# Expert rows turned by DMA transposes as two float16 numbers, instead of by TensorE

## The chip, the cores and the metric

The kernel runs on one core of one Trainium2 chip. The metric is the device time of one execution in microseconds (us), smaller being better. Engines are named as in the profile: PE is TensorE (PEld its weight loads), DVE is VectorE, ACT is ScalarE, POOL is GpSimd, SP is SyncE. `L1262` is line 1262 of the kernel.

## The reference: what is computed

Two layers on 4096 nodes of 256 features. Each layer adds graph attention (one round in the first layer, two in the second) and then a feed-forward part to its input, each on normalised rows. The change lies in the last part alone, a mixture of six experts of which each row takes its best two:

```
rh = relu(features @ router_w1 + router_b1)
expert_logits = softmax(rh @ router_w2 + router_b2)
top_w, top_i = top_k(expert_logits, 2)
routing_weights = softmax(top_w)
h1 = relu(features @ expert_w1[e] + expert_b1[e])
h2 = relu(h1 @ expert_w2[e] + expert_b2[e])
expert_out = h2 @ expert_w3[e] + expert_b3[e]
x = x + sum over the two chosen e of expert_out * routing_weights
```

All inputs are float32; weights of an expert are three 256 x 256 matrices.

## The kernel before

The program is one long sequence of stages: an attention layer with mask making, a feed-forward stage of 30 steps (from about 814 to 1793 us), two more attention layers (to about 3087), a router (to about 3162), the expert loop (to about 3392), and a last pass that gathers the results and adds them up. Instructions outside the attention loops and the feed-forward stage are ordered by a scheduler, engine by engine, when the program is built: the order in the source is a wish, the data and the buffers of the pools decide.

**Router** (L987 to L1215). In eight groups of 512 rows it normalises rows, writes them to a DRAM table `nd` (L1015), transposes them on TensorE, and computes the six logits (L1001, L1024). In between SP issues the loads of the expert weights, `ew` (L1036). VectorE then makes from the logits a list: the 8192 pairs of row and expert, grouped by expert into T = 37 tiles of TR = 256 places. `source` says which row of `nd` stands in each place, `dest` where its result goes in the DRAM table `yd`, `expert` which expert a tile belongs to.

**Expert loop** (L1305 to L1325), over the 37 tiles. For tile i:

- `gather` (L1224): two indirect DMAs, issued by POOL, bring 2 x 128 rows of `nd` into `gx` (four buffers).
- `turn` (L1234): four float32 transposes on TensorE into PSUM (`pt`), and one VectorE copy to `xT` (L1241), 128 x 512.
- `fetch` (L1243): the tile's expert number goes into registers of PE, DVE and ACT, and the weights of layers one and two are copied from `ew` to `w0` (VectorE) and `w1` (ScalarE), both L1255, 128 x 512, three buffers each.
- `hidden(i, 0)` (L1257): four float32 matmuls (each is two records in the trace), then bias and relu by ScalarE in two halves (L1273) to `h0`.
- `hidden(i, 1)`: the same with `w1`, bias and relu by VectorE (L1275) to `h1`.
- `result` (L1277): four float32 matmuls with `ew[2]`, the addition of the bias by VectorE into `ye` (L1291, three buffers), and two indirect DMAs by POOL to `yd` (L1293).

In the built order TensorE runs, from tile to tile: second product of i, first product of i+1, last product of i, transposes of i+2. POOL has the gathers of seven tiles ahead of the first scatter and then takes gathers and scatters in turn. Each POOL DMA waits for the eighth before it to have landed.

**The feed-forward stage** is not changed, but it holds the operations that the change uses. Half of its product is made from pairs of float16 numbers: ScalarE rounds the scaled numbers to float16 (L852), VectorE subtracts that from the scaled numbers and rounds what is left (L853), a DMA transpose issued by SP turns both halves at once (L857), and TensorE multiplies every half of the rows with every half of the weights (L899), while the other half of its columns is float32 (L896).

## Time and profile before

| | us |
|---|---|
| median of 3 runs | 3432.09 (3427.78 to 3432.75) |
| the profiled execution's own time | 3432.09 |
| its span, first to last instruction | 3430.3 |
| TensorE, busy in the span | 3156.7 (92%) |
| VectorE | 3115.3 (91%) |
| ScalarE | 2754.3 (80%) |
| GpSimd | 1242.3 (36%) |
| first gather issued | 3162.7 |
| first product of tile 0 begins | 3170.0 |
| last scatter issued | 3392.0 |

How to read the lines that follow. A group line reads: line, engine, operation, output <- inputs, shape, count, then busy us and mean ns of one, then the idle time of the engine just before these instructions and what ended it. Timeline lines begin with start and length in us. Matmuls are pipelined: the start of the next tells more than the modelled end. TensorE's granted clock is 1.00 through the whole expert loop and 0.50 in most of the second half of the router.

### The profile page before, as it was taken

To read this page: it belongs to the slowest core of one execution; us is meant where nothing else is said; L and a number is where in the kernel's file an instruction comes from. 1 tells how busy PE (TensorE), PEld (TensorE's weight loads), DVE (VectorE), ACT (ScalarE), POOL (GpSimd) and SP (SyncE) were. 2 spreads that over 40 slices of the span, in tenths; PEclk is the share of its full clock that TensorE was granted. 3 is DMA by queue.
4 is the path that set the end of the run, shared out by engine and by line. 5 is a ranking of instruction groups with operands and counts; after the bars stand their busy time and mean duration, and the time that the engine had idled before them with its cause. 6 is when DMAs were issued, how large, how long until landed. Compare 5 with 4: busy or idle time off the path is not lost.

```text
span 3430.3 us, 84143 instructions
## 1 busy us (share of the span) xinstructions
PE 3156.7 (92%) x34367; PEld 2771.3 (81%) x34367; DVE 3115.3 (91%) x6016; ACT 2754.3 (80%) x3414; POOL 1242.3 (36%) x1149
## 2 busy tenths in 40 slices
PE   7889999996999999999988999999989999985995
PEld 4788888884888888888876999999779999983884
DVE  7999999998999999999988999999889999996445
ACT  3888888896888888888866999999799999982221
POOL 3211100003999999999992000000200000002662
PEclk9999999997999999999999999999999999996997
DMA  7997886603333333333354031230503041314224
GB/s 146 173 228 152 184 184 142 192 22 77 68 67 68 69 69 69 69 69 68 67 140 147 22 123 58 90 118 24 167 24 124 27 136 43 120 46 145 88 91 185
DMA packets 533658, 351.62 MB, mean 103 GB/s; under 512 B 350589, under 2 KB 483866, under 8 KB 533274
## 3 DMA queue, kind: packets, MB, share of 16 engines
q1 hardware_dynamic: 452210, 287.12, 30.4%
q0 software_dynamic: 73920, 52.97, 9.9%
q10 hardware_dynamic: 7144, 6.16, 0.6%
q8 instruction: 271, 4.44, 0.5%
q14 instruction: 113, 0.93, 0.1%
HBM read 248.01 MB, written 68.81 MB: 92 GB/s over the span
## 4 chain that ended last, share of the span: by engine, by line
PE 36%; DVE 35%; issue 13%; POOL 7%; ACT 6%; DMA 2%; DVEq 0%; POOLq 0%; ACTq 0%; SPq 0%
DVE m L617 17%; PE acc L569 10%; PE po L899 9%; PE po L896 9%; ACT st L483 4%; DVE rows L632 3%; PE tp L831 2%; DVE m L632 2%; POOL th L862 2%; PE ph L1262 1%; POOL yd L1293 1%; DVE z_st L874 1%; DVE y L838 1%; POOL gx L1227 1%; DVE u L496 1%
## 5 line engine op out<-in xcount | busy, mean ns | idle before, releaser
L569 PE MATMUL acc<-vals,m 128*128 128x130 f16 (+1 forms) x19456 | 1722.4, 233 | 72.0 <-DVE m L632 42.5
L483 ACT ACTIVATE st<-f1b,f2b 128x1024 bf16<-128x1024 f32 (+2 forms) x1664 | 1659.1, 1073 | 98.8 <-DVE m L617 92.1
L569 PEld LDWEIGHTS <-m 128*128 128x128 bf16 x19456 | 1517.3, 98 | 170.2 <-DVE m L632 64.8
L617 DVE TENSOR_TENSOR m<-st,m 128x2048 bf16<-128x2048 bf16 (+2 forms) x832 | 929.1, 1134 | 15.2 <-ACT st L483 14.9
L569 PE MATMUL acc<-vals,rows 128*128 128x130 f16 x5120 | 614.1, 221 | 15.1 <-DVE rows L632 15.1
L899 PE MATMUL po<-w,zT 128*128 128x256 f16 x3840 | 580.4, 274 | 5.7 <-DMA zT<-z 5.7
L896 PE MATMUL po<-wT,zT 128*128 128x256 f32 x1920 | 579.1, 384 | 6.4 <-ACT zT L881 6.4
L862 POOL TENSOR_TENSOR th<-th,y 128x1024 f32<-128x1024 f32 x240 | 568.8, 2370 | 38.4 <-ACT th L861 14.8
L899 PEld LDWEIGHTS <-zT 128*128 128x128 f16 x3840 | 377.6, 98 | 169.7 <-DMA zT<-z 7.3
L569 PEld LDWEIGHTS <-rows 128*128 128x128 bf16 x5120 | 490.0, 96 | 20.5 <-DVE rows L632 20.1
L632 DVE TENSOR_TENSOR rows<-m,m 128x2048 bf16<-128x2048 bf16 x320 | 391.7, 1224 | 10.2
L838 DVE SCALAR_TENSOR_TENSOR y<-po,z_rs,bias 128x256 f32<-128x256 f32 x928 | 384.8, 477 | 4.2 <-PE po L899 2.1
L874 DVE BATCH_NORM_STATS2 z_st<-z 128x6 f32<-128x256 f32 x960 | 335.5, 412 | 0.0
L896 PEld LDWEIGHTS po<-wT,zT 128*128 128x128 f32 x1920 | 292.5, 193 | 16.4 <-ACT zT L881 7.8
L106 POOL TENSOR_TENSOR ln_rstd<-ln_rstd,mhalf 128x4 f32<-128x4 f32 x32 | 42.1, 1317 | 656.8 <-DVE ln_rstd L105 641.9
L850 ACT ACTIVATE z<-th 128x1024 f32<-128x1024 f32 x240 | 251.2, 1046 | 7.3 <-POOL th L862 6.6
L209 POOL DMA_DIRECT2D rows<-in_adj_dram x80 | 72.9, 912 | 492.9 <-PE tp_m L219 479.4
L861 ACT ACTIVATE th<-y 128x1024 f32<-128x1024 f32 x240 | 249.8, 1041 | 0.1
L885 POOL TENSOR_TENSOR z_rs<-z_rs,mhalf 128x4 f32<-128x4 f32 x240 | 244.5, 1019 | 0.0
L881 ACT COPY zT<-tp 128x512 f32<-128x512 f32 x240 | 140.8, 587 | 116.2 <-PE tp L831 116.2
L632 DVE TENSOR_TENSOR m<-m,m 128x1792 bf16<-128x1792 bf16 (+1 forms) x200 | 202.2, 1011 | 13.0 <-PE acc L569 0.5
L462 POOL MEMSET hs<- 128x4 f32 x3 | 0.3, 103 | 582.4 <-DVE u L513 582.3
(246 smaller groups left out, 3159.1 us busy)
## 6 DMA issues: line engine op xcount, KB each, us to landing
m<-edges SPq DMA_DIRECT2D x32, 2048.0 KB
rows<-in_adj_dram POOLq DMA_DIRECT2D x64, 448.0 KB
edges<-ms SPq DMA_DIRECT2D x64, 448.0 KB
m<-edges SPq DMA_DIRECT2D x16, 1792.0 KB
f1b<-fd SPq DMA_DIRECT2D x32, 512.0 KB
rows<-x1d SPq DMA_DIRECT2D x16, 512.0 KB
y<-yd SPq DMA_DIRECT2D x16, 512.0 KB
f1b<-fd SPq DMA_DIRECT2D x16, 448.0 KB
```

Source lines behind the costliest of these rows:

```text
L483: nc.scalar.activation(steps[at][:, s, :w], f1b[c, h][:, :w], AF.Relu, bias=f2b[:, 2 * q + s, h : h + 1], scale=BIG)
L569: nc.tensor.matmul(acc[:, i, cols], lhs[:, s, rows], v[:, cols], start=(j == 0 and n_ == 0), stop=(j == NT - 1 and n_ == 1), skip_group_ch ...
L617: nc.vector.tensor_tensor(m1[:, :, :w], st[:, :, :w], m, OP.logical_and if turned(q) else OP.min)
L632: nc.vector.tensor_tensor(m2[:, :, :w], m, m1[:, :, :w], OP.subtract)
L838: nc.vector.scalar_tensor_tensor(y[:, g * G + r, :], po[:, r, :], rstd[:, r : r + 1], last if end else bias, op0=OP.mult, op1=OP.add,)
L850: nc.scalar.activation(z, th.pop(u), AF.Silu, scale=0.01)
L861: nc.scalar.activation(th[at], y[:, g * G : (g + 1) * G, :], AF.Tanh, scale=0.01)
L862: ins = nc.gpsimd.tensor_tensor(th[at], th[at], y[:, g * G : (g + 1) * G, :], OP.add)
L874: nc.vector.bn_stats(st[:, r, :], z[:, r, :])
L885: nc.gpsimd.tensor_tensor(rs[u], rs[u], mhalf, OP.pow)
L896: nc.tensor.matmul(po[:, r, :], src[:, r * P : (r + 1) * P], wT, start=True, stop=False)
L899: nc.tensor.matmul(po[:, r, :], src16[:, part * G + r, :], w16[:, other, :], start=False, stop=(part == 1 and other == 1),)
```

## The change

It is confined to the router's set-up and the expert loop.

- Router: the greatest absolute value of the first layer's weights is found (six reductions of 128 x 512 on VectorE, a transpose and a small matmul on TensorE, five small VectorE instructions). From its exponent come two powers of two in `wscale`: one by which weights are scaled ahead of the rounding, one that takes that scale and the rows' scale of 2^10 out again.
- `turn`: no TensorE transposes, no copy of `xT`. ScalarE writes the scaled rows, rounded to float16, into the first half of `x16`; VectorE writes what the rounding left into the second half; SP issues one DMA transpose of all 128 x 1024 numbers into `xT`. `x16` has three buffers, `xT` four. PSUM's pool for the transposes goes.
- `fetch`: ScalarE and VectorE make two float16 halves of the first layer's weights in the same way, in place of VectorE's copy; the copy of the second layer's weights stays.
- `hidden(i, 0)`: sixteen float16 matmuls of 128 x 256 in place of four float32 ones (two halves of rows by two of weights, by two parts of the inner sum, by two of the output); relu takes `wscale` as its scale.
- The loop: `gather` is asked for three tiles ahead in place of two, with five `gx` buffers in place of four; `turn` two tiles ahead in place of one.

```diff
+            far = rone.tile([P, E + 1], F32, name="far")
+            for e in range(E):
+                nc.vector.tensor_reduce(
+                    far[:, e : e + 1],
+                    ew[0][:, e].rearrange("p k c -> p (k c)"),
+                    axis=AX.X, op=OP.max, apply_absolute_value=True,
+                )
+            nc.vector.tensor_reduce(far[:, E:], far[:, :E], axis=AX.X, op=OP.max)
+            ps = bank("ps_s")
+            nc.tensor.transpose(ps[:1, :P], far[:, E:], ident)
+            big = rone.tile([1, 1], F32, name="big")
+            nc.vector.tensor_reduce(big, ps[:1, :P], axis=AX.X, op=OP.max)
+            ps = bank("ps_s")
+            nc.tensor.matmul(ps[:, :1], ones[:1, :], big, start=True, stop=True)
...
         def gather(i):
-            rows[i] = work.tile([P, 2, C], F32, name="gx", bufs=4)
+            rows[i] = work.tile([P, 2, C], F32, name="gx", bufs=5)
...
         def turn(i):
             src = rows.pop(i)
-            pt = ps_t.tile([P, KC, TR], F32, name="pt")
-            for k in range(KC):
-                for r in range(2):
-                    nc.tensor.transpose(pt[:, k, r * P : (r + 1) * P], src[:, r, k * P : (k + 1) * P], ident)
-            xT[i] = work.tile([P, KC, TR], F32, name="xT")
-            nc.vector.tensor_copy(xT[i], pt)
+            x16 = work.tile([P, 2, 2, C], F16, name="x16")
+            nc.scalar.activation(x16[:, 0], src, AF.Copy, scale=ZS)
+            nc.vector.scalar_tensor_tensor(x16[:, 1], src, ZS, x16[:, 0], op0=OP.mult, op1=OP.subtract)
+            xT[i] = work.tile([P, 8, P], F16, name="xT", bufs=4)
+            nc.sync.dma_start_transpose(xT[i], x16.rearrange("p s r c -> p (s r c)"))
...
         def fetch(i):
...
-            held[i] = []
-            for layer, copy in enumerate((nc.vector.tensor_copy, nc.scalar.copy)):
-                held[i].append(work.tile([P, KC, C], F32, name=f"w{layer}"))
-                copy(held[i][layer], ew[layer][:, bass.DynSlice(which[i], 1)].rearrange("p o k c -> p (o k) c"))
+            w16 = work.tile([P, 2, KC, C], F16, name="w0")
+            nc.scalar.activation(w16[:, 0], first, AF.Identity, scale=wscale[:, :1])
+            nc.vector.scalar_tensor_tensor(
+                w16[:, 1], first, wscale[:, :1], w16[:, 0], op0=OP.mult, op1=OP.subtract
+            )
+            held[i] = [w16, work.tile([P, KC, C], F32, name="w1")]
+            nc.scalar.copy(held[i][1], second)
 
         def hidden(i, layer, src):
...
+            if layer == 0:
+                src = src.rearrange("p (s r k) n -> p s k r n", s=2, k=KC)
+                ops = [(w[:, v, k], src[:, u, k]) for k in range(KC) for v in range(2) for u in range(2)]
+            else:
+                ops = [(w[:, k], src[:, k]) for k in range(KC)]
...
-        gather(0)
-        gather(1)
+        for i in range(3):
+            gather(i)
         for i in range(T + 1):
-            if i + 2 < T:
-                gather(i + 2)
+            if i + 3 < T:
+                gather(i + 3)
             if i < T:
                 if i == 0:
                     fetch(0)
                     turn(0)
+                    turn(1)
...
-            if i + 1 < T:
-                turn(i + 1)
+            if i + 2 < T:
+                turn(i + 2)
```

In the prediction, "high half" is ScalarE's rounding and "low half" VectorE's rest; `h0` and `h1` are the outputs of the first two products; "first", "second" and "last product" of a tile are `hidden(i, 0)`, `hidden(i, 1)` and the matmuls of `result(i)`.

## The prediction

> **What bounds the kernel now.** The edit touches one stage at the end, so I first placed that stage in the chain of work that ended last, then took busy times in stretches of it. From 3186 to 3386 us the expert loop runs steadily (stretch, its length, then busy time and count of PE, PEld, DVE, ACT, POOL, then granted clock, DMA share, GB/s):
>
> ```profile
> 3236.00:3286.00 50.00, 49.01 (x240) 41.87 (x239) 21.95 (x43) 12.77 (x27) 34.13 (x35) 1.00 0.28 92
> 3286.00:3336.00 50.00, 48.62 (x238) 41.25 (x237) 22.71 (x44) 12.28 (x25) 32.97 (x34) 1.00 0.27 88
> ```
>
> TensorE is 98% busy at full clock; VectorE and ScalarE are under half. The order of time on TensorE (start, length) gives the price of a tile; `ph<-xT` is the first product, `ph<-h` the second, `po` the last, `pt` the transposes:
>
> ```profile
> 3201.75 1.89 PE L1283 MATMUL po<-ew,h 128*128 x8
> 3203.48 0.60 PE L1239 MATMUL pt<-ident,gx 128*128 128x128 f32 x4
> 3203.91 1.89 PE L1262 MATMUL ph<-h,w 128*128 128x256 f32 x8
> 3206.08 1.99 PE L1262 MATMUL ph<-xT,w 128*128 128x256 f32 x8 [0.27 <-DVE xT L1241]
> 3207.91 1.89 PE L1283 MATMUL po<-ew,h 128*128 x8
> 3209.63 0.60 PE L1239 MATMUL pt<-ident,gx 128*128 128x128 f32 x4
> 3210.07 1.89 PE L1262 MATMUL ph<-h,w 128*128 128x256 f32 x8
> 3211.80 1.89 PE L1262 MATMUL ph<-xT,w 128*128 128x256 f32 x8
> 3213.53 0.81 PE L1283 MATMUL po<-ew,h 128*128 x3
> ```
>
> Read the starts, since ends overlap. A product of four float32 matmuls (eight records) holds TensorE 1.73 us (3211.80 to 3213.53), four transposes 0.43 (3203.48 to 3203.91). A tile is 3 x 1.73 + 0.43 = 5.62 us (3207.91 to 3213.53); every other tile adds 0.54 for transposes that are copied late (3201.75 to 3207.91 is 6.16). From the end of tile 1's last product (3186.46) to that of tile 36 (3389.41) are 202.95 us. POOL is the near second: 1.27 to 1.35 us from one DMA issue to the next, four a tile, about 5.3 (busy us and mean ns, then idle before and what ended it):
>
> ```profile
> L1293 POOL DMA_INDIRECT yd<-ye,dest x67 | 67.4, 1006 | 27.1 <-issue 16.0 <-DVE ye L1291 6.5 <-DVE xT L1241 4.6
> L1227 POOL DMA_INDIRECT gx<-nd,source x60 | 59.0, 982 | 38.9 <-PE pt L1239 21.1 <-issue 17.8
> L1255 ACT COPY w<-ew 128x512 f32 x32 | 19.8, 618 | 93.8 <-PE ph L1262 48.4 <-issue 45.4
> L1255 DVE COPY w<-ew 128x512 f32 x31 | 15.3, 493 | 36.2 <-PE ph L1262 36.2
> ```
>
> The new operations stand in the feed-forward stage, which does the same trick on tiles of the same shape:
>
> ```profile
> 1700.16 0.60 PE L899 MATMUL po<-w,zT 128*128 128x256 f16 x4
> 1700.59 0.60 PE L896 MATMUL po<-wT,zT 128*128 128x256 f32 x2
> ```
>
> and, with least, median and most ns of one,
>
> ```profile
> L852 ACT ACTIVATE z<-z,scale x240: 721/722/724, 818.6 to 1777.2; 128x512 f16<-128x512 f32 x120
> L853 DVE SCALAR_TENSOR_TENSOR z<-z,scale,z x240: 741/742/2062, 819.3 to 1778.9; 128x512 f16<-128x512 f32 x120
> L857 SPq DMA_TRANSPOSE zT<-z x240: 1232/1233/2364, 820.1 to 1784.7; - x120
> ```
>
> Four float16 passes hold TensorE 0.43 us, 0.109 each. The transpose occupies SP 1.23 us, but by the trace's semaphore records it is 3.04 us from issue to the sixteenth landing (median of 240; least 3.01; 4.43 at the 95th per cent and 5.37 at most, where bulk loads share its queue).
>
> **What the Trainium skill says.** "TensorE: Matmul & The Clock Gate", Back-to-back issue gap: an isolated warm matmul takes N/2.4 + 2.5 ns, 109 ns for N = 256; the 0.109 here agrees. Same page, What's actually happening: an idle window of about 3.4 us halves the clock. Agrees: it is 0.5 from 3126.9 to 3174.6. "DMA: Bandwidth & Descriptors", Queues, rings and completion order: each DMA engine takes turns between queues by whole packets. The trace of before never has a transpose beside an indirect DMA, so it can't confirm it. "SBUF — State Buffer", SBUF: two separate sides: a float32 SBUF copy on VectorE locks the port by which GpSimd writes descriptors. Agrees in size: POOL's issue takes 0.945 us while VectorE does little (3173 to 3177), 0.98 to 1.01 in the loop.
>
> **The change part by part**, per tile unless said.
>
> 1. TensorE. Four transposes go: -0.43, and the 0.54 stall of every second tile. The first product becomes 16 float16 passes: 16 x 0.109 = 1.74 against 1.73, nothing. New floor: 1.73 + 1.73 + 1.74 = 5.20.
>
> 2. ScalarE gains two roundings. The weights' takes 0.72 (L852's row). The rows' has no strided source: between the 0.59 of a plain 128x512 copy (L881) and 0.72; I take 0.66. In all 0.84 + 0.72 + 0.66 + 0.62 = 2.84 of 5.2. VectorE loses xT (0.68) and the copy of w (0.49) and gains two subtractions, 0.74 by L853, 0.68 by the float32 one of L673; I take 0.70 for the rows': 3.0 a tile. As work both are hidden under TensorE. Their order is not.
>
> 3. The new ring. In the built program's order VectorE has, per tile i: h1(i), weights' low half (i+4), ye(i), rows' low half (i+8). ScalarE has h0(i), weights' high (i+3), rows' high (i+7), w1(i+3). The three x16 buffers make the rows' high half of tile i+8 wait for the transpose of tile i+5; the four xT buffers make that wait until the first product of tile i+1 is done. Behind the waiting ScalarE instruction stand w1(i+4) and h0(i+2); behind VectorE's stand h1(i+1), and TensorE's last product (i+1) waits for it. SP has nothing else queued. From the end of the first product (i+1): to SP 0.30 (ScalarE's h0 started at 3267.01 where TensorE's next product started at 3266.75: 0.26), transpose 3.04, to ScalarE 0.10, high half 0.66, to VectorE 0.06, low half 0.70, first half of h1 0.48 less 0.08 overlap, to TensorE 0.06: 5.32. Then last product (i+1), second (i+2), first (i+2 to i+3): 5.20. That is two tiles in 10.52, 5.26 a tile. So the ring is longer than TensorE's work even with a quiet transpose.
>
> 4. The transpose beside gathers and scatters, not shown before. A gather is 32 packets of 4 KB, two per DMA engine at 0.2 us each (L1227's and L1293's DMA share 0.27 over 4 per tile gives 0.4 us each). Bounds: nothing extra (3.04), or as under bulk loads (4.43). It cannot be below nothing: extra traffic doesn't speed it. During its 1.4 us of moving bytes POOL starts about one DMA, so I take +0.4: two tiles in 10.92, 5.46 each. The ring applies to last products 2 to 29 (rows end at 37): 28 x 5.46 = 152.9; then six at 5.20 and 4.2 for the last (before: 3385.21 to 3389.41): 188.3. Against 202.95: **-14.6**.
>
> 5. Gathers three ahead, five buffers. The built order puts 26 gathers ahead of the first scatter (before: 14). 26 x 1.25 from 3162.75 ends near 3195; three ye buffers cover it, since ye(3) is due after 3200. POOL needs 4 x 1.25 to 1.30 = 5.0 to 5.2: under 5.46. Without that cover POOL would set 5.3.
>
> 6. Start of the loop. Row gathers land at 3167.05 and then every 2.5 us (before's trace). ScalarE's order puts the high halves of tiles 0 to 5 ahead of h0(0). Tile 5 lands near 3179.6, so h0(0) ends near 3181.1; the second product (0) began at 3174.8 before. VectorE's h1(0) also stands behind tile 6 (lands near 3182), h1(1) behind tile 8 (near 3187). Tile 1's last product then ends near 3191.1 instead of 3186.46: +4.6; with the 5 us gap cooling the clock near 3193.1: +6.7. Taken: **+5.6**.
>
> 7. Router. Six 128x512 reductions (0.67 by L160's) on VectorE, in gaps that GpSimd's power leaves or beside TensorE's chain; the transpose of far makes TensorE's router product (6) wait for VectorE, about 0.9. All exposed would be 4 + 0.9; all but that wait hidden 0.9. Taken **+1.2**. The scaling is ready 35 us before use: free, covered by routing.
>
> Sum: -14.6 + 5.6 + 1.2 = -7.8. The profiled execution took 3432.09, 1.79 round its span of 3430.3, and equals the median: 3424.3, say **3424**.
>
> **Rivals.** (a) The ring has slack, TensorE sets 5.20: for it, the transposes in the FFN keep to 3.04, hand-overs may be shorter; against, the queue order. 28 x 0.26 less: 3417. (b) *Slower*: gathers and scatters stretch the transpose, at one place, T between x16 and xT. Every 1 us adds 0.5 x 28 = 14 us. It breaks even at 3.04 + 0.4 + 7.8/14 = 4.0 us, and is slower by 0.2% (6.9 us, about what a measurement here can tell from no change) from 4.5; at 4.6, 3440. For it: 4.43 under bulk; against: only 0.27 of DMA time is taken. (c) A wash: TensorE gets its 0.7 a tile back and the ring returns it, at 5.6 to 5.75 a tile (192.2 to 196.4 in place of 188.3), with a cold start and up to 3.7 more in the router: 3429 to 3437.
>
> **How the numbers follow.** Forecast 0.50, its own range 3420 to 3429, three fifths of it faster by over 0.2% (0.30), the rest within (0.20). (a) 0.17, faster. (c) 0.13, within. (b) 0.20, slower. So faster 0.47, within 0.33, slower 0.20. Leaving out little below 3414 and half of (b)'s tail above 3440 gives 3414 to 3440.
>
> **What would show it.** Right: TensorE's last products 5.4 to 5.5 us apart, waiting 0.2 to 0.3 on VectorE's h (L1314); ScalarE's x16 waiting on the transpose; transposes landing 3.3 to 3.6 us after issue; TensorE idle near 3176 to 3181; last seven tiles at 5.2. Wrong: transposes at 4 us or over (b), no wait ahead of the last product (a), POOL without gaps.

## The result, and the profile after

The changed kernel takes 3462.13 us in the median of six runs (3459.25 to 3473.58), the kernel before 3432.85 beside it (3427.78 to 3434.89): ratio 1.0095, 95% interval 1.0077 to 1.0114. It is slower by about 1%, outside the forecast range. The profiled execution took 3459.25, its span is 3457.5, so 27.2 more than before.

The same two stretches of the expert loop, in the changed kernel (stretch, length, then busy time and count of PE, PEld, DVE, ACT, POOL, granted clock, DMA share, GB/s):

```profile
3236.00:3286.00 50.00, 43.40 (x240) 34.58 (x240) 22.30 (x38) 20.58 (x37) 30.90 (x31) 0.97 0.47 121
3286.00:3336.00 50.00, 44.40 (x271) 37.00 (x269) 22.52 (x39) 21.77 (x40) 33.20 (x33) 1.00 0.53 127
```

TensorE, 98% busy before, is now busy 87 and 89%: it has less work a tile and waits more. The order of time on TensorE shows where:

```profile
3211.41 2.00 PE L1322 MATMUL po<-ew,h 128*128 x8 [1.70 <-DVE h L1314]
3213.24 1.89 PE L1301 MATMUL ph<-h,w 128*128 128x256 f32 x8
3214.97 1.91 PE L1301 MATMUL ph<-xT,w 128*128 128x256 f16 x16
3216.72 1.89 PE L1322 MATMUL po<-ew,h 128*128 x8
3218.45 1.89 PE L1301 MATMUL ph<-h,w 128*128 128x256 f32 x8
3220.17 1.91 PE L1301 MATMUL ph<-xT,w 128*128 128x256 f16 x16
3223.54 2.06 PE L1322 MATMUL po<-ew,h 128*128 x8 [1.46 <-DVE h L1314]
```

Sixteen float16 passes hold TensorE 1.75 us (3214.97 to 3216.72), as forecast, and every second tile waits for VectorE's `h1` ahead of its last product, as forecast; but the wait is 1.5 to 1.7 us in these lines (0.7 to 1.7 in tiles 2 to 8) and not 0.2 to 0.3. The groups of the loop from 3186 to 3386 (busy us and mean ns, then idle before and what ended it):

```profile
L1332 POOL DMA_INDIRECT yd<-ye,dest x60 | 61.5, 1026 | 58.0 <-DVE ye L1330 45.5 <-issue 12.5
L1256 POOL DMA_INDIRECT gx<-nd,source x56 | 57.8, 1032 | 21.6 <-issue 17.4 <-DVE x L1267 4.2
L1285 DVE SCALAR_TENSOR_TENSOR w<-ew,wscale,w 128x512 f16<-128x512 f16 x31 | 23.3, 751 | 64.6 <-ACT w L1284 39.6 <-PE po L1322 12.4 <-ACT h L1312 10.4
L1284 ACT ACTIVATE w<-ew,wscale 128x512 f16 x31 | 22.2, 716 | 0.0
L1267 DVE SCALAR_TENSOR_TENSOR x<-gx,x 128x512 f16<-128x512 f32 x30 | 20.8, 694 | 31.3 <-ACT x L1266 17.9 <-DMA gx<-nd,source 6.9 <-issue 6.4
L1266 ACT ACTIVATE x<-gx 128x512 f16<-128x512 f32 x30 | 18.9, 630 | 56.7 <-DMA xT<-x 44.0 <-DMA gx<-nd,source 9.8 <-DVE ye L1330 2.9
```

The prices are those of the forecast (0.716 and 0.630 on ScalarE, 0.751 and 0.694 on VectorE), and the rows' high half waits for the transpose, 44.0 us in 200. Where the loss lies, from the starts of the last products (tile 0, 1, 27, 36):

| | before | after |
|---|---|---|
| first gather issued | 3162.75 | 3161.59 |
| tile 0's last product starts | 3178.8 | 3192.6 |
| tile 1's | 3184.6 | 3204.3 |
| tile 27's | 3337.4 | 3367.6 |
| tile 36's | 3387.7 | 3413.7 |
| mean from tile 1 to 27 | 5.88 | 6.28 |

The start loses 19.7 us, tiles 1 to 27 another 10.5, and the last nine win 4.2 back (eight at 5.2 to 5.3 us, the last at 4.2). Two things lie behind this: the first 27 tiles wait for slow transposes (step 4 below), and at the start something else, which is seen nowhere in the forecast. All engines of the changed kernel, 3181 to 3199 us (PE's weight loads and most of POOL's rows left out):

```profile
3181.00 3.78 PE L1301 MATMUL ph<-h,w 128*128 128x256 f32 x8 [4.29 <-ACT h L1312]
...
3184.58 1.72 PE L1301 MATMUL ph<-xT,w 128*128 128x256 f16 x10
...
3187.80 0.94 POOL L1256 DMA_INDIRECT gx<-nd,source  x1 [0.30 <-issue]
3189.05 0.94 POOL L1256 DMA_INDIRECT gx<-nd,source  x1 [0.30 <-issue]
3190.30 0.94 POOL L1256 DMA_INDIRECT gx<-nd,source  x1 [0.30 <-issue]
3191.54 0.94 POOL L1256 DMA_INDIRECT gx<-nd,source  x1 [0.30 <-issue]
3192.08 0.62 ACT L1289 COPY w<-ew 128x512 f32 x1 [8.61 <-remote]
3192.08 0.88 DVE L1314 TENSOR_SCALAR h<-ph,bsel 128x256 f32<-128x256 f32 x2 [7.89 <-remote]
...
3192.62 3.54 PE L1322 MATMUL po<-ew,h 128*128 x8 [6.31 <-DVE h L1314]
...
3198.47 1.02 ACT L1312 ACTIVATE h<-ph,bsel,wscale 128x256 f32<-128x256 f32 x2 [5.24 <-remote]
```

Tile 0's second product has ended by 3184.8. VectorE's relu and ScalarE's copy wait for nothing but that, and start together 7.3 us later. The profile finds no releaser ("remote"), because at that moment nothing ends: TensorE's count, which both wait for, is raised only then (3192.05 by the trace's semaphore records). Tile 1's first product ends at 3186.3; its relu and the next transpose start, and VectorE's wait for it ends, all at 3198.46, 12.1 us later. From here on I call this a **late signal**. In the stretch from 3160 us to the last product, 15 of TensorE's 92 recorded raises come over 0.1 us after their product's end; of VectorE's 154 and ScalarE's 133 none does. In the kernel before it is 34 of 114 (at most 1.9 us), again TensorE's only, and in its earlier stages none.

The waits cost clock as well. In the kernel before, TensorE's granted clock is 1.00 from 3174.6 us to the end of the loop. In the changed kernel it falls to 0.50 from 3178.7, 3188.9, 3199.2 and 3270.9 us on, for 3.4 to 6.8 us each, every time in or right after a wait of TensorE of 2.8 to 6.3 us; tile 0's last product, `3192.62 3.54` above, takes 3.54 us in the trace in place of 1.89.

### The profile page after: what moved, and what is told of

Its sections match the earlier page's. It is cut to its first block, busy times and chain, and to the rows that moved or that the text cites. A ratio compares the mean times of both kernels' runs of the same rounds, so it can differ in the third digit from the quotient of the medians.

```text
span 3457.5 us, 84712 instructions
## 1 busy us (share of the span) xinstructions
PE 3148.4 (91%) x34518; PEld 2757.6 (80%) x34518; DVE 3127.8 (90%) x6028; ACT 2804.0 (81%) x3488; POOL 1244.5 (36%) x1149
## 4 chain that ended last, share of the span: by engine, by line
DVE 35%; PE 34%; issue 14%; POOL 7%; ACT 6%; DMA 3%; another core or an unknown queue 0%; DVEq 0%; POOLq 0%; ACTq 0%
DVE m L617 17%; PE acc L569 10%; PE po L899 9%; PE po L896 9%; ACT st L483 4%; DVE rows L632 3%; PE tp L831 2%; DVE m L632 2%; POOL th L862 2%; POOL yd L1332 1%; POOL gx L1256 1%; DVE z_st L874 1%; DVE y L838 1%; PE ph L308 1%; DVE u L496 1%
## 5 line engine op out<-in xcount | busy, mean ns | idle before, releaser
L632 DVE TENSOR_TENSOR rows<-m,m 128x2048 bf16<-128x2048 bf16 x320 | 391.7, 1224 | 10.2
```

The costliest lines, as they stand in the source:

```text
L632: nc.vector.tensor_tensor(m2[:, :, :w], m, m1[:, :, :w], OP.subtract)
```

## The experiments

Two theories at the beginning. **Ring**: the transpose and its buffers set the pace, at more than the forecast 5.46 us. **Late signals**: TensorE's signals come late while POOL issues indirect DMAs. Later the chip itself came into it: the runs fell on three chips of the kind, called A, B and C here; each ratio is to the kernel before on the same chip (3432 to 3433 on A, 3437 on B, 3421 on C). The chip of the first measurement isn't on record; its 3432.85 for the kernel before fits A. "Late" counts TensorE's recorded raises over 0.1 us late, in the stretch named above, with the largest. The lateness is counted from the last product that had ended before the raise, so it is a least value: by this count the changed kernel's 12.1 us are only 5.8. "Tile" is the mean from tile 1's to tile 27's last product.

| run | chip | us | ratio, 95% interval | tile | late |
|---|---|---|---|---|---|
| ring6 | A | 3471.89 | 1.0118 (1.0101 to 1.0135) | 6.38 | 23 of 95, 10.2 |
| tight | A | 3455.35 | 1.0078 (1.0062 to 1.0095) | 6.35 | 23 of 96, 4.2 |
| plain_in | A | 3434.52 | 1.0010 (1.0004 to 1.0017) | 6.11 | 5 of 99, 0.3 |
| pe_fixed | A | 3466.87 | 1.0102 (1.0085 to 1.0119) | 6.69 | 23 of 103, 4.4 |
| pool_plain | A | 3443.01 | 1.0038 (1.0028 to 1.0049) | 6.24 | 6 of 102, 0.3 |
| deep | A | 3464.14 | 1.0093 (1.0076 to 1.0111) | 6.45 | 51 of 102, 9.5 |
| b_deep | A | 3433.36 | 1.0006 (0.9997 to 1.0015) | 5.92 | 31 of 113, 1.5 |
| b_ahead3 | A | 3435.01 | 1.0006 (1.0000 to 1.0013) | 5.89 | 37 of 118, 5.7 |
| no_turn | B | 3463.07 | 1.0076 (1.0060 to 1.0093) | 6.54 | 33 of 106, 6.3 |
| plain_out | B | 3422.18 | 0.9957 (0.9941 to 0.9974) | 6.20 | 2 of 101, 9.5 |
| n16 | B | 3471.37 | 1.0097 (1.0081 to 1.0114) | 7.09 | 38 of 101, 6.8 |
| b_plain_in | B | 3416.02 | 0.9941 (0.9924 to 0.9957) | 5.62 | 0 of 142 |
| no_turn_plain | C | 3404.74 | 0.9949 (0.9933 to 0.9966) | 5.20 | 0 of 111 |
| paced | C | 3440.81 | 1.0051 (1.0033 to 1.0068) | 5.82 | 0 of 111 |
| b_f16 | C | 3422.44 | 1.0005 (0.9996 to 1.0014) | 5.64 | 0 of 148 |
| b_paced | C | 3421.89 | 1.0000 (0.9992 to 1.0009) | 5.62 | 0 of 148 |
| after_again | B | 3468.83 | 1.0092 (1.0078 to 1.0106) | 6.86 | 21 of 95, 9.8 |
| b_paced_again | B | 3441.46 | 1.0014 (1.0007 to 1.0020) | 6.23 | 49 of 130, 1.6 |

Names that begin with `b_` are the kernel before with one edit; the others are the changed kernel with one (no_turn_plain with two, after_again with none; b_f16 is the first product's part of the change alone). The four whose gathers are plain need not wait for the routing, so part of their time is won ahead of the loop (`b_plain_in`: tile 1's last product 11.1 us earlier than before): of these the tile column is read, not the total.

**ring6**

```diff
-            x16 = work.tile([P, 2, 2, C], F16, name="x16")
+            x16 = work.tile([P, 2, 2, C], F16, name="x16", bufs=6)
...
-            xT[i] = work.tile([P, 8, P], F16, name="xT", bufs=4)
+            xT[i] = work.tile([P, 8, P], F16, name="xT", bufs=6)
```

> Six x16 and six xT buffers in place of three and four, nothing else. Ring theory (the turned rows' buffers set the pace): last products of tiles 1 to 27, 6.28 us apart in the changed kernel, come down to 5.2 to 5.4, some 23 to 29 us less; the longer run-ahead at the start (nine rows' high halves ahead of the first relu instead of six) gives back up to 8: 3440 to 3447. Late-signal theory (TensorE's end-of-product signals reach the other engines 2 to 7 us late while POOL's gathers are under way): buffers don't touch that, and more gathers run back to back at the start; 3455 to 3470.

Measured 3471.89, above both. More buffers do not help: tile 0's last product starts at 3207.0, behind signals up to 10.2 us late, and the tiles take 6.38 us. As the whole of the loss the ring is out.

**tight**

```diff
-            rows[i] = work.tile([P, 2, C], F32, name="gx", bufs=5)
+            rows[i] = work.tile([P, 2, C], F32, name="gx", bufs=4)
...
-            x16 = work.tile([P, 2, 2, C], F16, name="x16")
+            x16 = work.tile([P, 2, 2, C], F16, name="x16", bufs=2)
...
-            xT[i] = work.tile([P, 8, P], F16, name="xT", bufs=4)
+            xT[i] = work.tile([P, 8, P], F16, name="xT", bufs=2)
...
-        for i in range(3):
-            gather(i)
+        gather(0)
+        gather(1)
...
-            if i + 3 < T:
-                gather(i + 3)
+            if i + 2 < T:
+                gather(i + 2)
```

> Two x16 and two xT buffers, four gx buffers and gathers two ahead, so that four rows' high halves stand ahead of the first relu instead of six and about 18 gathers ahead of the first scatter instead of 26. Ring theory: a shorter ring in buffers, each transpose now waits for the first product two tiles back; 6.3 us a tile or more, 3465 to 3490. Run-ahead theory (what was lost is lost at the start, behind rows that are not needed yet): tile 1's last product starts 10 us or more earlier than 3204, total 3440 to 3450. Late-signal theory: fewer gathers back to back at the start, so the 13 us of late signals there shrink as well; 3435 to 3450.

Tile 1's last product starts at 3187.9, 16 us earlier than in the changed kernel, so what is lost at the start depends on how much is queued ahead there. The tiles take 6.35 us: the loop keeps its loss, and the total is 3455.

**plain_in**

```diff
-                nc.gpsimd.indirect_dma_start(out=rows[i][:, r, :], ..., in_=nd[:, :], in_offset=...)
+                lo = (2 * i + r) * P % (N - P)
+                nc.sync.dma_start(rows[i][:, r, :], nd[lo : lo + P, :])
```

> The rows come by plain loads on SP's queue, in order, in place of the indirect gathers: this leaves out the choice of rows, the bytes are the same. Late-signal theory with POOL's indirect DMAs as the cause: signals of TensorE's products are on time (at most 0.1 us) but for those beside scatters; the start gains 13 us and the steady tiles about 0.4 us each; 3425 to 3440. Ring or run-ahead theory: the queues' order is the same, so 6.0 to 6.3 us a tile stay; 3450 to 3460 (SP's loads ahead of its transposes may even add).

Inside the range of the late-signal theory, and the late signals are gone (0.3 us at most). But the tiles still take 6.11 us in place of 6.28, so there is a second cause.

**pe_fixed**

```diff
-                engines=[mybir.EngineType.PE, mybir.EngineType.DVE, mybir.EngineType.Activation],
+                engines=[mybir.EngineType.DVE, mybir.EngineType.Activation],
...
-            w = ew[2][:, bass.DynSlice(which[i], 1)]
+            w = ew[2][:, i % E : i % E + 1]
```

> TensorE's last product takes expert i mod 8 at a fixed address, so TensorE neither loads a register nor computes an address in the loop: this leaves out the choice of the third weight. If TensorE's register load holds up its signals: no signal later than 0.1 us, 3430 to 3440. If POOL's indirect DMAs do, or the ring is the bound: no change, 3455 to 3465.

3466.87, just above the range for no change, with signals at least 4.4 us late: TensorE's register loads are not the reason.

**pool_plain**: as plain_in, with `nc.gpsimd.dma_start` in place of `nc.sync.dma_start`.

> The rows come by POOL's own plain loads, in order, on the queue where the indirect gathers stood: this leaves out the choice of rows; POOL's order and the bytes are the same. If any load that POOL issues makes TensorE's signals late: as in the changed kernel, signals up to 6 us late, 3450 to 3465. If only the indirect ones do: signals on time but for those beside scatters, tile 1's last product near 3192 to 3195, 3425 to 3437.

Signals are on time, with POOL still loading and still scattering; so it is not any load by POOL. The start shows what that is worth:

```profile
3178.12 3.78 PE L1297 MATMUL ph<-h,w 128*128 128x256 f32 x8 [4.98 <-ACT h L1308]
...
3181.94 0.88 DVE L1310 TENSOR_SCALAR h<-ph,bsel 128x256 f32<-128x256 f32 x2 [0.73 <-PE ph L1297]
3183.26 1.89 PE L1318 MATMUL po<-ew,h 128*128 x8
...
3189.67 1.56 PE L1318 MATMUL po<-ew,h 128*128 x6 [1.05 <-DVE h L1310]
```

The relu starts 0.04 us after the product ends (3181.9). From the start of tile 0's second product to that of tile 1's last one are 11.55 us (3178.12 to 3189.67); in the changed kernel, with the same order, 23.35 (3181.00 to 3204.35): a difference of 11.8 us. That late signals are the whole of it is argued from the two timelines, since the plain loads also bring rows earlier. The total lies above the range, since the tiles take 6.24 with no signal over 0.3 us late: beside the plain loads the transposes get slower too, up to 6.2 us from issue to the next high half.

```profile
3250.55 1.23 SPq L1265 DMA_TRANSPOSE xT<-x  x1
...
3256.74 0.63 ACT L1262 ACTIVATE x<-gx 128x512 f16<-128x512 f32 x1 [4.49 <-DMA xT<-x]
```

So plain_in and pool_plain say what late signals cost at the start; in the loop they say only that something else holds the tiles at over 6 us when signals are on time.

**deep**

```diff
-        for i in range(T + 1):
+        for i in range(T + 2):
...
-            h = hT.pop(i, None)
-            if i:
-                hT[i - 1] = last_h
-                result(i - 1)
+            if 1 <= i <= T:
+                hidden(i - 1, 1, hT.pop(i - 1))
+            if i >= 2:
+                result(i - 2)
             if i + 2 < T:
                 turn(i + 2)
-            if i < T:
-                hidden(i, 1, h)
-                last_h = hT.pop(i)
```

> The changed kernel with one more tile between the products: in each step the first product of tile i, the second of i - 1, the last of i - 2. Each relu then has 5.2 us before TensorE needs it in place of 1.7. Late-signal theory: the signals stay as late as before, but all up to 5 us are hidden; steady tiles at 5.2 to 5.4, the start still late by 6 to 12 us: 3420 to 3440. Ring theory (transposes and their buffers set the pace): no help, 6.0 to 6.3 a tile, 3450 to 3465.

The number is the ring theory's, its reason is not: up to five tiles in a row at 5.2 to 5.7 us are followed by one or two of 6.2 to 12.6, and every second recorded signal is late, by 9.5 us and more. Slack of 5 us is used up by still later signals.

**b_deep**: the same edit in the kernel before (`turn(i + 1)` stays).

> The kernel before with the same extra tile between the products. If the 0.54 us lost at every second tile there is a late signal and not late work: tiles at 5.62 us throughout, 3.5 to 8.6 us less, 3423 to 3429. If it is a bound of POOL or of the copies: no change, 3430 to 3436.

No change: 5.92 us a tile, signals up to 1.5 us late. This did not tell late signals from a bound of POOL.

**b_ahead3**

```diff
-            rows[i] = work.tile([P, 2, C], F32, name="gx", bufs=4)
+            rows[i] = work.tile([P, 2, C], F32, name="gx", bufs=5)
...
-        gather(0)
-        gather(1)
+        for i in range(3):
+            gather(i)
...
-            if i + 2 < T:
-                gather(i + 2)
+            if i + 3 < T:
+                gather(i + 3)
```

> The kernel before with five row buffers and gathers three tiles ahead, that part of the change alone. By the prediction it is free: 3429 to 3435. Late-signal theory: four more gathers back to back at the start of the loop, so 0 to 5 us more: 3432 to 3438.

That part alone costs 0.06%, near nothing; yet one signal at the start is 5.7 us late (1.9 at that place before), and tile 1 is 1.8 us later. So a longer train of gathers goes with a later signal in float32 products too; it is one signal in one run.

**no_turn**

```diff
-            x16 = work.tile([P, 2, 2, C], F16, name="x16")
+            x16 = work.tile([P, 2, 2, C], F16, name="x16", bufs=6)
...
-            xT[i] = work.tile([P, 8, P], F16, name="xT", bufs=4)
-            nc.sync.dma_start_transpose(xT[i], x16.rearrange("p s r c -> p (s r c)"))
+            xT[i] = x16.rearrange("p s r (k n) -> p (s r k) n", n=P)
```

> The changed kernel without the DMA transposes: the first product takes the two halves of the rows as they lie (this leaves out the turning), from six x16 buffers. Ring theory: the transposes beside gathers (3.9 us on average from issue to the next high half, in place of 3.4 forecast) cost about half a us a tile; without them the steady tiles take 5.2 to 5.6: 3440 to 3448. Late-signal theory: the late signals of TensorE are there with or without transposes, start at 3204 as in the changed kernel and 5.6 to 6.1 a tile: 3446 to 3458.

3463.07, above both. Without any transpose one to three tiles at 5.2 to 5.3 us are followed by one of 6.3 to 11: TensorE is free of the ring, and late signals (6.3 us and more) take the ring's place.

**plain_out**

```diff
-                ins = nc.gpsimd.indirect_dma_start(out=yd[:, :], out_offset=..., in_=y[:, r, :], in_offset=None)
+                lo = (2 * i + r) * P % yd.shape[0]
+                ins = nc.gpsimd.dma_start(yd[lo : lo + P, :], y[:, r, :])
```

> The scatters are plain stores that POOL issues, to rows in order (this leaves out where the results belong); the indirect gathers stay. If the gathers alone make TensorE's signals late: late by 2 to 9 us at the start and as in the changed kernel later, 3450 to 3465. If POOL's whole load of four indirect DMAs a tile does: the start as in the changed kernel (only gathers run there), but few late signals after 3206, 3438 to 3448.

With gathers alone in flight, at the start, signals come 8.0 and 9.5 us late as before the edit; after that, with two indirect DMAs a tile in place of four, none does. The total is lower than expected for another reason: the last pass need not wait for the last of the plain stores, and its loads run beside tiles 20 to 27, which take up to 8.3 us. The loop ends at 3414.9, against 3415.7. Ahead of that the loop shows the ring by itself, 69.1 us from tile 5's last product to tile 17's, 5.76 each. One turn of it:

```profile
3239.04 1.00 POOL L1256 DMA_INDIRECT gx<-nd,source  x1 [0.30 <-DVE h L1314]
3239.66 0.38 PE L1301 MATMUL ph<-xT,w 128*128 128x256 f16 x2
...
3240.08 12.67 SPq L1269 DMA_TRANSPOSE xT<-x  x3
...
3240.34 0.99 POOL L1256 DMA_INDIRECT gx<-nd,source  x1 [0.30 <-issue]
...
3244.14 0.63 ACT L1266 ACTIVATE x<-gx 128x512 f16<-128x512 f32 x1 [2.37 <-DMA xT<-x]
...
3244.80 0.69 DVE L1267 SCALAR_TENSOR_TENSOR x<-gx,x 128x512 f16<-128x512 f32 x1 [1.64 <-ACT x L1266]
...
3245.41 0.87 DVE L1314 TENSOR_SCALAR h<-ph,bsel 128x256 f32<-128x256 f32 x2
...
3245.94 2.07 PE L1322 MATMUL po<-ew,h 128*128 x8 [0.69 <-DVE h L1314]
```

First product ends, transpose issued (3240.08), next high half 4.06 us later, low half, relu, last product at 3245.94: the forecast chain link by link. The transposes alternate: 4.06 from issue to high half when a gather is issued 0.3 us after them, about 3.2 when the nearest comes 0.5 us after them (tiles 10 to 22). The one on the chain is always the slow one, since the tile that waits is the one whose transpose meets the gathers. Put into the forecast's sum, 10.52 - 3.14 + 4.06 = 11.44 for two tiles (3.14 is the forecast's 3.04 and its 0.10 to ScalarE); measured 11.5.

**n16**

```diff
-        nd = dram.tile([N, C], F32, name="nd")
+        nd = dram.tile([N, 2 * C], F16, name="nd")
...
+                    nc.scalar.activation(n16[:, :, 0], n, AF.Copy, scale=ZS)
+                    nc.vector.scalar_tensor_tensor(n16[:, :, 1], n, ZS, n16[:, :, 0], op0=OP.mult, op1=OP.subtract)
-                    nc.sync.dma_start(runs_of(nd, u), n)
+                    nc.sync.dma_start(runs_of(nd, u), n16.rearrange("p g s c -> p g (s c)"))
...
-            rows[i] = work.tile([P, 2, C], F32, name="gx", bufs=5)
+            rows[i] = work.tile([P, 2, 2, C], F16, name="x16", bufs=5)
...
-            nc.sync.dma_start_transpose(xT[i], x16.rearrange("p s r c -> p (s r c)"))
+            nc.sync.dma_start_transpose(xT[i], src.rearrange("p r s c -> p (r s c)"))
```

> The rows are split once each in the router stage (4096 rows, not 9472), the halves are stored as pairs of float16 in the same 1 KB a row, gathered as such and turned straight from the gather's buffer: no high or low half of rows stands on ScalarE's or VectorE's queue in the loop. Ring theory: relus no longer stand behind a transpose, so 5.2 to 5.4 a tile from the start, 2 to 6 us more in the router: 3420 to 3432. Late-signal theory: TensorE is never held back by the ring, its signals come later still (as with the extra tile between the products), 5.8 to 6.4 a tile: 3440 to 3460.

Above even the late-signal range. Its engines from 3251 to 3259 us:

```profile
3251.74 1.67 PE L1303 MATMUL ph<-h,w 128*128 128x256 f32 x7
...
3253.25 1.91 PE L1303 MATMUL ph<-xT,w 128*128 128x256 f16 x16
...
3258.12 0.88 DVE L1316 TENSOR_SCALAR h<-ph,bsel 128x256 f32<-128x256 f32 x2 [2.17 <-remote]
...
3258.18 0.62 ACT L1291 COPY w<-ew 128x512 f32 x1 [6.40 <-remote]
3258.66 1.56 PE L1324 MATMUL po<-ew,h 128*128 x6 [3.50 <-issue]
```

The second product ends near 3253.4; its relu, with nothing ahead of it on VectorE from 3255.95 on, starts at 3258.12, together with ScalarE's copy, and the last product at 3258.66. No relu stands behind a transpose here. This and no_turn say that on these chips taking the ring away alone gains nothing clear (3471 and 3463, the changed kernel itself 3469 on B).

**b_plain_in**: the edit of plain_in in the kernel before.

> The kernel before with plain loads of rows on SP's queue in place of the gathers (leaves out the choice of rows). Late-signal theory: the 0.54 us of every second tile was a late signal too, not late work; tiles at 5.62 throughout and no signal over 0.3 us late: 3420 to 3427. If it was late work (transposes that are copied late, as the prediction had it): no change, 3430 to 3434.

Every tile takes 5.62 us, no signal is late. The total is below the range by what is won ahead of the loop.

**no_turn_plain**: plain_in and no_turn together.

> The changed kernel without the transposes and with plain loads of the rows on SP's queue (leaves out the turning and the choice of rows): neither the ring nor the four indirect DMAs a tile. If these two are all that kept the tiles from 5.20 us: tiles 1 to 27 at 5.2 to 5.3 us, no signal over 0.3 us late, 3410 to 3418. If something else adds: 5.6 or more, 3425 and up.

Every tile takes 5.20 us. TensorE, in two stretches:

```profile
3190.00:3240.00 50.00, 50.00 (x312) 43.50 (x311) 27.16 (x50) 25.78 (x47) 20.54 (x20) 1.00 0.32 97
3240.00:3290.00 50.00, 50.00 (x305) 43.53 (x304) 26.01 (x48) 27.05 (x49) 19.73 (x19) 1.00 0.33 105
```

100% busy at full clock: with both edits nothing stands between the changed kernel and TensorE's floor. It ran on chip C, where the kernel before takes 3421, hence a total below the range; and since no run on C has a late signal, it can't tell what the gathers' edit was worth here.

**paced, b_f16, b_paced**

```diff
 paced
+                nc.gpsimd.memset(rows[i][:, r, :], 0.0)
                 nc.gpsimd.indirect_dma_start(
 b_paced
+                nc.gpsimd.memset(rows[i][:, r, :1], 0.0)
                 nc.gpsimd.indirect_dma_start(
 b_f16 (from the changed kernel)
-            xT[i] = work.tile([P, 8, P], F16, name="xT", bufs=4)
-            nc.sync.dma_start_transpose(xT[i], x16.rearrange("p s r c -> p (s r c)"))
...
+            xT[i] = work.tile([P, 2, KC, TR], F16, name="xT")
+            nc.scalar.activation(xT[i][:, 0], pt, AF.Copy, scale=ZS)
+            nc.vector.scalar_tensor_tensor(xT[i][:, 1], pt, ZS, xT[i][:, 0], op0=OP.mult, op1=OP.subtract)
...
```

b_f16 also has the kernel before's transposes into `pt`, its gathers two ahead with four buffers and its `turn` one ahead; those lines are left out here.

> The changed kernel with a clearing of the row buffer on POOL ahead of each gather, so that POOL's indirect DMAs are less dense: some 0.3 to 0.6 us of other POOL work for each gather; all values as before. If the density of indirect DMAs makes TensorE's signals late: lateness at the start falls from 7 us to under 2 and mostly goes from the tiles, which POOL then sets at 5.8 to 6.2 us: 3440 to 3452. If their number a tile does, or the gathers themselves: signals as late as in the changed kernel and POOL's extra time on top, 3460 to 3475.

> One part alone: the first product from halves of rows and weights, with the rows still turned by TensorE and split from PSUM, gathers two ahead, four row buffers. TensorE has 5.64 us of work a tile. If the sixteen passes cost what the prediction says (the same as four float32 ones) and the late signals are those of the kernel before: 5.9 a tile, 3431 to 3438. If the many short passes make the signals later: 6.1 or more a tile, 3440 to 3455.

> The kernel before with a clearing of one column of the row buffer on POOL ahead of each gather, 0.1 to 0.2 us of other POOL work each; all values as before. If density of indirect DMAs makes the signals late and this is enough: the 0.54 us at every second tile goes or shrinks, 3423 to 3430. If not: 3431 to 3440, POOL's time showing.

None of the three has one late signal, and that is no proof of what they were built for: the kernel before itself takes 3421 on this chip, b_paced the same (1.0000), so chip C seems to have none to take away (all runs on it come from one session). What the runs do show: the sixteen passes cost what four float32 ones do (5.64 a tile against 5.62), and the changed kernel's order with signals on time takes 5.82 us a tile where POOL has 0.33 us of clearing for each gather on top.

**after_again, b_paced_again**: the changed kernel and b_paced, unchanged.

> The changed kernel unchanged, once more, since on the chip of the four runs before the kernel before took 3421 us and no signal of TensorE was late. If this chip has late signals (before at 3430 or more): as known, ratio 1.008 to 1.011. If it has none (before near 3421): what is left is the ring at 5.7 us a tile up to the end of the rows and the start behind rows not yet needed (tile 1's last product some 5 us late): ratio 1.000 to 1.003, which makes the late signals three quarters or more of the loss.

> The kernel before with a clearing of one column of each row buffer on POOL ahead of the gathers, once more. On a chip with late signals: if the density of indirect DMAs makes them late and this is enough, tiles at 5.62 us, ratio 0.997 to 0.998; if the number of indirect DMAs or something else does, 0.54 us more at every second tile as before, ratio 0.999 to 1.002. On a chip without late signals: 0.999 to 1.001 either way, which settles nothing.

Chip B has late signals. The changed kernel's ratio is as known, 1.0092, with tiles at 6.86. The very same b_paced, in the same two stretches, first on C, then on B:

```profile
3236.00:3286.00 50.00, 50.00 (x249) 43.99 (x248) 22.87 (x45) 14.08 (x27) 35.99 (x54) 1.00 0.29 94
3286.00:3336.00 50.00, 50.00 (x251) 44.11 (x250) 23.31 (x45) 14.03 (x27) 36.13 (x54) 1.00 0.30 94
```

```profile
3236.00:3286.00 50.00, 46.03 (x222) 38.47 (x220) 20.47 (x40) 11.38 (x23) 32.53 (x49) 1.00 0.26 85
3286.00:3336.00 50.00, 47.21 (x228) 40.19 (x229) 22.06 (x43) 12.81 (x26) 32.83 (x50) 1.00 0.25 82
```

TensorE is 100% busy on C and 92 to 94% on B, at the same granted clock, with the same program. A pause of one small POOL instruction doesn't take the late signals away; with it the kernel before is slower by 0.14%. No version that beats both kernels came out of this.

## Why the prediction was wrong, step by step

From -7.8 forecast to +27.2 in the span are 35.0 us: 15.3 at the start, 20.9 in the loop, -2.4 in the router, 1.2 behind the loop (from the start of tile 36's last product to the end 42.6 us before, 43.8 after). Two steps failed: step 4, the transpose beside gathers, which is the larger part of the loop's loss, and step 6, where TensorE's signals were taken to arrive at once.

1. **TensorE's floor, 5.20**: right. Tiles 31 to 35 take 5.20, and so do all of no_turn_plain but the last. Wrong in it was the "0.54 stall of every second tile for transposes that are copied late". It was a late signal. In the kernel before:

```profile
3202.60 1.24 POOL L1227 DMA_INDIRECT gx<-nd,source  x1 [0.30 <-issue]
3204.73 0.69 DVE L1291 TENSOR_TENSOR ye<-po,b 128x512 f32<-128x512 f32 x1 [1.76 <-PE pt L1239]
3205.34 0.68 DVE L1241 COPY xT<-pt 128x512 f32<-128x512 f32 x1
```

TensorE had gone on from its last product at 3203.48 and from the transposes at 3203.91, both lines shown in the prediction; VectorE sat idle for both until 3204.73. I read the wait by the engine that it names and did not set its end against the end of what it waits for. With plain gathers (b_plain_in) the stall is gone with all transposes still on TensorE. So of the 0.70 us a tile that the forecast took off TensorE, only 0.43 were the change's to take.

2. **Prices of the new operations**: right, within 0.03 us each. ScalarE's relu with a scale from memory takes 0.56 a half (0.47 before), not forecast.

3. **The ring, two tiles in 10.52 with a quiet transpose**: right in form. plain_out shows the chain link by link.

4. **The transpose beside gathers, +0.4**: mis-sized, and this is the failed step behind most of the loop's loss. In plain_out it is +0.9 on the chain (4.06 against 3.14), because the tile that waits is the one whose transpose meets the gathers. In the changed kernel it is more. Tiles 1 to 9 (3204.3 to 3252.6 us) show it free of late signals: no recorded raise there is over 0.05 us late, and every transpose is issued within 0.05 us of the end of the first product. Yet these tiles take 6.04 us each. One turn of the ring:

```profile
3216.91 1.29 SPq L1269 DMA_TRANSPOSE xT<-x  x1
3217.20 0.99 POOL L1256 DMA_INDIRECT gx<-nd,source  x1 [0.30 <-issue]
3218.50 0.96 POOL L1256 DMA_INDIRECT gx<-nd,source  x1 [0.30 <-issue]
3221.74 0.63 ACT L1266 ACTIVATE x<-gx 128x512 f16<-128x512 f32 x1 [3.13 <-DMA xT<-x]
3222.40 0.69 DVE L1267 SCALAR_TENSOR_TENSOR x<-gx,x 128x512 f16<-128x512 f32 x1 [2.41 <-ACT x L1266]
3223.01 0.87 DVE L1314 TENSOR_SCALAR h<-ph,bsel 128x256 f32<-128x256 f32 x2
```

From issue to the next high half are 4.83 us here; the four transposes on the chain of tiles 1 to 9 take 5.07, 4.83, 4.56 and 4.03, those between them 3.3 to 3.5. With each of these in place of 3.14 in the forecast's own sum of 10.52 for two tiles, the sum is 12.45, 12.21, 11.94 and 11.41; measured 12.37, 12.19, 12.07 and 11.65. If the whole ring ran like this, it would be 28 x (6.04 - 5.46) = 16.2 of the 20.9 us, an estimate. So rival (b) was right in place and size: their mean, 4.62, less the 0.10 to ScalarE is the 4.5 from which it has the change slower. Tiles of 6.04 are also slower than the 5.62 of the kernel before with its signals on time.

5. **Gathers ahead are free**: alone they are (b_ahead3, 0.06%). That POOL's issue takes longer in the loop (0.945 us against 0.98 to 1.01) is measured; that VectorE's copies are the reason is tested by no run here.

6. **Start of the loop, +5.6**: the queue order was right: `h0` of tile 0 ends at 3181.4, where I had 3181.1. But the signals of the next two products come 7.3 and 12.1 us late: this is the other failed step, since the forecast had put 0.06 to 0.30 us between the end of one engine's work and the start of what waits for it. pool_plain, whose signals are on time, is 11.8 us faster there; 15.3 are missing in all, and the cause of the other 3.5 is open.

7. **Router, +1.2**: wrong in sign, the first gather is issued 1.2 us earlier.

What is left of the loop's 20.9 us, about 5, has a cause in the trace: signals due at 3252.8, 3265.8, 3312 and 3343 came 0.5 to 3.8 us late, with ScalarE's relu and the next transpose waiting, and the clock at 0.50 after the second. That their cost is the whole rest is argued, not shown. The two bounds hide each other: with signals on time but slow transposes the tiles take 6.11 and 6.24 (plain_in, pool_plain), without transposes but with late signals 6.54 (no_turn) and 7.09 (n16), and only without either 5.20 (no_turn_plain, on C).

Neither forecast nor any rival had late signals. Rival (b) named the right place for the larger part of the loop's loss. That the whole change is slower even with all signals on time isn't shown: the changed kernel never ran on C. An estimate: 28 tiles 0.20 to 0.42 slower (5.82 in paced and 6.04 in tiles 1 to 9, against 5.62), seven 0.42 faster, the start 9 longer (from the first gather to tile 1's last product 30.9 us in pool_plain, 21.8 in the kernel before), the router 1 earlier: 10 to 17 us slower.

Open: what holds TensorE's signals; why it is not seen on chip C; and why they are up to 12.1 us late in the changed kernel and 1.9 in the one before. Longer trains of gathers go with it (26 ahead of the first scatter, 14 before; b_ahead3). Whether the sixteen short passes do, b_f16 was to tell, and it ran where no signal is late. One suspect that no run clears is the recording itself. Every execution here was recorded (each has a span and a granted clock), and where signals are late, records of raises are missing too: in the kernel before 34 of TensorE's 148 in the loop and none of 1651 ahead of it; in b_paced 18 of 148 on B and none on C. Missing records alone don't make signals late (plain_in lacks 13 of 112). How late signals are when nothing is recorded is not known.

## What to carry to other kernels

A wait in the profile has two ends: set the waiter's start against the end of what it waited for, and where they are over 0.1 us apart, don't count on the named engine's work to shorten it. A transpose or load in a ring of buffers meets other DMAs in step with the loop, so the one on the chain can be the slow one each time: take the slow value, not a mean. In a loop with four indirect DMAs a tile, replace one kind by plain DMAs of the same bytes: one run tells whether signals were late. What is then left isn't free of the edit's own effect, since the plain loads slowed the transposes too (pool_plain). And where two bounds hide each other, taking one away shows little: look for tiles in which only one of them is at work, as tiles 1 to 9 here.

## What the runs showed of the hardware

- In recorded executions TensorE's end-of-product signals can reach other engines late: 12.1 us in the changed kernel, while no recorded one of VectorE or ScalarE was over 0.01 us. Seen on two of three chips and only in the expert loop; in steady tiles over 0.3 us late only where POOL's gathers and its scatters were both indirect, and plain gathers (plain_in, pool_plain) or plain stores (plain_out) were enough to end it. At the start it is there with gathers alone in flight (9.5 us in plain_out).
- When held signals come, they come one after another, 0.09 us apart in the changed kernel (3198.443 and 3198.536; 3269.580 and 3269.672). The Trainium skill ("TensorE: Matmul & The Clock Gate", The cost: per-tile semaphore tail) says that increments are written one after another, 26 ns each; that agrees in kind, but the step here is 92 ns, and that it is the same thing isn't shown.
- A DMA transpose of 128 x 1024 numbers takes 3.1 to 3.2 us from issue to the next step that needs it when quiet, 4.06 when an indirect gather is issued 0.3 us after it (plain_out, tiles 10 to 22), 4.0 to 5.3 for the slow ones with gathers and scatters indirect (changed kernel, tiles 2 to 22), and 6.19 in pool_plain with two plain loads. The Trainium skill ("DMA: Bandwidth & Descriptors", Queues, rings and completion order) has queues share each DMA engine by whole packets; the stretch fits that, the runs don't prove it.
